# The clamp inside an elu of an elu, moved from VectorE to ScalarE as relu(1 - q)

## The chip, the cores and the metric

The kernel runs on one core of one Trainium2 chip. The metric is the device time of one execution in microseconds (us); three runs of the kernel before gave a median of 2963.7 us (2962.96 to 2964.57). The engines have short names in the profile: PE is TensorE's matmuls, PEld its weight loads, DVE is VectorE, ACT is ScalarE, POOL is GpSimd and SP is SyncE, which only issues transfers.

## The reference

Four graph attention layers run over a batch of 32 graphs with 512 nodes and 256 features. Each layer normalizes its input, takes the relu and adds the attention's result to it. The fourth layer is the one that the change touches. Cut to what matters:

```python
def _gat(inp, adj_mask, W, a):
    ...                                   # leaky relu logits, mask, softmax
    h_prime = jnp.einsum('bij,bjf->bif', att, h)
    return jax.nn.elu(h_prime)
out = jax.nn.relu(jnp.matmul(x, mlp1_w) + mlp1_b)
residual = out
out = _gat(jax.nn.relu(out), None, W_fc, a_fc)
out = jax.nn.elu(out) + residual          # an elu of an elu
out = jax.nn.relu(jnp.matmul(out, mlp2_w) + mlp2_b)
residual = out
out = _gat(jax.nn.relu(out), adj, W_hand, a_hand)
out = jax.nn.elu(out) + residual          # and again
return jax.nn.relu(out)
```

For a positive z, elu(elu(z)) + 1 is z + 1. For a negative z it is exp(exp(z) - 1). Both together are max(z, 0) + exp(min(exp(z), 1) - 1).

## The kernel before

All tensors are fp32 (the adjacency mask is bf16). The 512 nodes of a graph lie in four tiles of 128 partitions. One graph is one batch step, written as a Python generator that goes through the four layers (`layer0` to `layer3`) and yields where it lets another graph in. Four graphs (`NS = 4`, "streams") are in work at once, each a quarter of a batch behind the next, and each owns two of the eight PSUM banks. A planner in Python picks the stream whose next piece is due first (`ready`, `after_us`), and so sets the program order. Then the Tile framework's scheduler, which has its own idea of how long instructions take, sets the order in each engine's queue within the data dependencies. [...]

In the steady part one batch step takes about 89 us of the core, and the order repeats after four batch steps (once for each stream), so there are four variants of a batch period.

The pieces of work that the prediction speaks of, with their lines in the profile:

- `norm`: statistics (L262, L263), reciprocal root on ScalarE (L265, L266), then the normalized tile `xn` on VectorE (L269 where the scale is applied later, L273 where it is applied at once). The matmul helper is L66 and the transpose helper L70. `turn_pair` transposes `xn` and copies it out with a relu (L283).
- `values`: projection matmuls, exponentials of the logits (L312, L315), scaled values `v` (L313 on ScalarE, L316 on VectorE). `weights` then transposes columns of `v` and forms the attention weights on VectorE (L346).
- `averages`: the aggregation matmuls and the reciprocal of the denominator (L364). After it, layer 0 has its elu (exponential L398, relu L399, sums L382 and L383), layer 1 a relu (L417) and an add into `x` (L421).
- layer 2 has four heads (L439, L440, L484, L491, L492).
- layer 3: linear layers (`linear_t`, copied out on ScalarE at L332), the values of the fully connected attention (L515, L516, matmuls with `WFC`). That attention is computed by sorting: rows are scattered (L594), summed up, written to a table and gathered again (L642), which gives `g`, combined on VectorE (L657). Four tiles per batch then take exponential L661, relu L662 and `elu2_plus1`, and are transposed in `mlp_in` and added to `oT` (L713). The last batch takes the plain attention instead (`attend`, L538, L539). The second attention ends with two pairs of tiles, each with exponential L686 and relu L687 twice, `elu2_plus1`, a transpose of `rT`, the sum L697, the relu L698 on ScalarE, and the add into `x` on GpSimd (L700), then the store (L701).

`elu2_plus1(r, q)` receives r = max(z, 0) and q = exp(z), both 128x512, and leaves the sum in r. It has three steps: the clamp (L387, VectorE), the second exponential with the constant -1 as its bias tile (L388, ScalarE), and the add (L389, VectorE). It runs 192 times: 124 times on gathered tiles, 4 times in `attend`, 64 times at the end of layer 3.

Of the kernel before, what the change touches and what calls it, by code (L numbers as in the profile page):

```python
# [19 lines left out]
FP = mybir.dt.float32  # L20
# [3 lines left out]
AF = mybir.ActivationFunctionType  # L24
OP = mybir.AluOpType
# [3 lines left out]
P = 128  # L29
# [6 lines left out]
def fast(ctx, tc, flag, x, adj, w0, a0, w1, a1, w2, a2, mlp1_w, mlp1_b, mlp2_w, mlp2_b,  # L36
         w_fc, a_fc, w_hand, a_hand, out):
    nc = tc.nc
# [12 lines left out]
    const = ctx.enter_context(tc.tile_pool(name="const", bufs=1))  # L51
# [28 lines left out]
    make_identity(nc, ident)  # L80
    eps = const.tile([P, 1], FP, name="eps")
    nc.vector.memset(eps, EPS)
    minus1 = const.tile([P, 1], FP, name="minus1")
    nc.vector.memset(minus1, -1.0)
    seen = const.tile([P, 5 * B], FP, name="seen")

    def load_x(b):
# [296 lines left out]

    def elu2_plus1(r, q):

        nc.vector.tensor_scalar(q, q, 1.0, None, op0=OP.min)  # L387
        nc.scalar.activation(q, q, AF.Exp, bias=minus1)  # L388
        nc.vector.tensor_tensor(r, q, r, op=OP.add)  # L389

    def layer0(xt, xn, rs, when):
# [126 lines left out]
    def attend(oT, b):  # L518
# [12 lines left out]
        for t in range(NT):  # L531
            y, q = pair(), pair("q")
            for c, n in ((0, F + 1), (1, F)):
                ps = bank()
                aggregate(ps[:, :n], wt, t, lambda j: halves[c][:, j, :n])
                if c == 0:
                    rd = reciprocal(ps[:, F:F + 1])
                nc.scalar.activation(q[:, c, :], ps[:, :F], AF.Exp, scale=rd)  # L538
                nc.scalar.activation(y[:, c, :], ps[:, :F], AF.Relu, scale=rd)  # L539
            elu2_plus1(y, q)  # L540
            ys.append(y)
            yield after_us(0)
            if t:
                mlp_in(oT, ys[t - 1], t - 1)
                yield after_us(0)
# [4 lines left out]
    def sort_attend(oT, b):  # L550
# [100 lines left out]
        for t in range(NT):  # L651
            yield landed
            y, q = pair(), pair("q")
            g = gs[t]
            z = g[:, :2 * C]
            tc.keep_in_program_order(
                nc.vector.scalar_tensor_tensor(z, z, ends[:, t, 2:3], g[:, 2 * C:], op0=OP.mult, op1=OP.add)  # L657
            )
            rd = reciprocal(z[:, F:F + 1])
            z = z.rearrange("p (c n) -> p c n", c=2)[:, :, :F]  # L660
            nc.scalar.activation(q, z, AF.Exp, scale=rd)  # L661
            nc.scalar.activation(y, z, AF.Relu, scale=rd)  # L662
            elu2_plus1(y, q)
            if t + 2 < NT:
                gather(t + 2)
            got.append(y)
            landed = after_us(3)
            when.append(after_us(4))
            if t == 0:
                continue  # L670
            yield when[t - 1]
            mlp_in(oT, got[t - 1], t - 1)
# [4 lines left out]
    def layer3(xt, xn, when, b):  # L677
        oT = yield from linear_t((yield from turned(xn, when)), WM1, b1, "oT", 2)
        yield from (attend if b >= B - 1 else sort_attend)(oT, b)
        rT = yield from linear_t(oT, WM2, b2, "rT", 2)  # L680
        v, wt = yield from plain(rT, WHA)
        for t0 in range(0, NT, 2):
            y, q = pair(), pair("q")
            for i in range(2):
                p, rd = averages(v, wt, t0 + i)
                nc.scalar.activation(q[:, i, :], p, AF.Exp, scale=rd)  # L686
                nc.scalar.activation(y[:, i, :], p, AF.Relu, scale=rd)  # L687
                yield after_us(0)
            elu2_plus1(y, q)
            p = bank()  # L690
            for i in range(2):
                for k in range(KF):
                    transpose(
                        p[:, (i * KF + k) * P:(i * KF + k + 1) * P], rT[:, k, (t0 + i) * P:(t0 + i + 1) * P], ident
                    )
            yf = y.rearrange("p a f -> p (a f)")
            nc.vector.scalar_tensor_tensor(yf, p, -1.0, yf, op0=OP.add, op1=OP.add)  # L697
            nc.scalar.activation(y, y, AF.Relu)  # L698
            xr = xt[:, t0:t0 + 2, :]
            nc.gpsimd.tensor_tensor(xr, xr, y, op=OP.add)  # L700
            nc.sync.dma_start(  # L701
                out[b, t0 * P:(t0 + 2) * P, :].rearrange("(t p) f -> p t f", p=P), xr
            )
            yield after_us(0)
# [462 lines left out]
@with_exitstack  # L1167
def kernel(ctx: ExitStack, tc: tile.TileContext, *args):
    nc = tc.nc
    keep = ctx.enter_context(tc.tile_pool(name="keep", bufs=1))  # L1170
    flag = keep.tile([1, 1], I32, name="flag")
    fast(tc, flag, *args)
    bad = nc.values_load(flag[0:1, 0:1], min_val=0, max_val=1)
    with tc.If(bad > 0):
        general(tc, *args)
# [27 lines left out]
```

## Time and profile before

| | before |
|---|---|
| median of 3 runs | 2963.7 us (2962.96 to 2964.57) |
| the profiled execution's own time | 2958.47 us |
| its span in the profile | 2956.8 us |
| mean granted TensorE clock | 0.994 |
| TensorE busy | 2870.2 us, 97% |
| VectorE busy | 2270.1 us, 77% |
| ScalarE busy | 1493.6 us, 51% |
| GpSimd busy | 496.9 us, 17% |

The span is the time from the first to the last instruction; the execution's own time has a little more around it, 1.7 us here. TensorE's busy time is not the same as TensorE at its best, since matmuls overlap and their ends are modelled; the starts of matmuls are recorded. A row of a group of instructions names line, engine, operation, output and inputs, the shape, the count, then the busy time and the mean of one, and the idle time of the engine just before them with what ended it. A row of the waits names who waited for whom, the total in us, how often, and the longest.

### The profile page before, as it was taken

The page shows a single profiled execution, that of the slowest core. Times are in us where ns is not written, and L with a number is a line of the kernel's source. Part 1 is how long each engine was busy: PE and PEld are TensorE (multiplying, and loading weights), DVE is VectorE, ACT ScalarE, POOL GpSimd, SP SyncE. Part 2 cuts the span into 40 slices and gives each one's busy share as a digit, 9 for nine tenths or more (in the row PEclk, how much of TensorE's full clock was granted, in tenths as well). Part 3 has the DMA queues.
Part 4 walks back from the last instruction along what each step waited for, and adds up shares of the span by engine and source line. Part 5 has one row for each costly group of instructions (what it writes and reads, how often), then busy time and mean ns, then how long its engine had stood idle before and what let it go on. Part 6 is the DMA issues. An engine that isn't in the chain of part 4 may idle for free.

```text
span 2956.8 us, 43040 instructions
## 1 busy us (share of the span) xinstructions
PE 2870.2 (97%) x15273; PEld 2335.9 (79%) x15273; DVE 2270.1 (77%) x5674; ACT 1493.6 (51%) x3790; POOL 496.9 (17%) x509
## 2 busy tenths in 40 slices
PE   7999999999999999999999999999999999999998
PEld 6777888778888877888778888778878788887765
DVE  4678878778878778878778778788778788787763
ACT  3444455554555544555544555545555544555444
POOL 0011122111122111122011221111221111221120
PEclk9999999999999999999999999999999999999999
DMA  3022233232232332232222232222232222332230
GB/s 93 18 95 94 81 100 115 82 99 98 83 101 96 99 101 89 83 110 96 99 94 87 87 115 92 96 95 88 91 115 90 96 95 81 101 115 73 93 115 16
DMA packets 192765, 270.88 MB, mean 92 GB/s; under 512 B 16992, under 2 KB 155550, under 8 KB 192544
## 3 DMA queue, kind: packets, MB, share of 16 engines
q1 hardware_dynamic: 162784, 169.76, 18.0%
q0 software_dynamic: 29760, 98.30, 9.8%
q8 instruction: 123, 2.02, 0.3%
q14 instruction: 98, 0.80, 0.1%
HBM read 152.62 MB, written 115.39 MB: 91 GB/s over the span
## 4 chain that ended last, share of the span: by engine, by line
PE 85%; DVE 9%; ACT 3%; issue 2%; DMA 1%; POOL 0%; SPq 0%; POOLq 0%; ACTq 0%; DVEq 0%
PE b L66 77%; PE b L70 8%; DVE st L262 2%; DVE xn L273 1%; DVE xn L269 1%; DVE y L697 1%; DVE v L316 1%; ACT rs L265 1%; DVE y L389 0%; DVE w L346 0%; DVE mv L263 0%; DVE x L421 0%; DVE tot L633 0%; ACT q L388 0%; DMA sums<-order 0%
## 5 line engine op out<-in xcount | busy, mean ns | idle before, releaser
L66 PE MATMUL b<-v,w 128*128 128x65 f32 (+1 forms) x7232 | 1218.1, 321 | 9.7 <-DVE w L346 8.2
L66 PEld LDWEIGHTS b<-v,w 128*128 128x128 f32 x7232 | 1052.9, 191 | 164.9 <-issue 40.8
L66 PE MATMUL b<-WFC,oT 128*128 128x256 f32 (+1 forms) x2048 | 499.7, 381 | 3.0 <-ACT ends L515 3.0
L66 PEld LDWEIGHTS b<-WFC,oT 128*128 128x128 f32 x2048 | 374.1, 190 | 51.3 <-ACT v L516 3.6
L66 PE MATMUL b<-W,hT 128*128 128x259 f32 (+1 forms) x1536 | 384.0, 388 | 0.8 <-DVE v L316 0.3
L346 DVE SCALAR_TENSOR_TENSOR w<-b,v,maskT 128x512 f32<-128x512 f32 x512 | 369.8, 743 | 4.9 <-PE b L70 4.9
L594 POOL DMA_INDIRECT order<-v,at x248 | 280.3, 1130 | 467.5 <-DVE w L346 159.8
L66 PEld LDWEIGHTS b<-W,hT 128*128 128x128 f32 x1536 | 285.7, 192 | 47.0 <-ACT hT L283 2.3
L346 DVE SCALAR_TENSOR_TENSOR w<-spread,v,maskT 128x512 f32<-128x512 f32 x384 | 269.4, 741 | 0.5 <-DMA spread<-row 0.5
L364 DVE RECIPROCAL rden<-b 128x1 f32<-128x1 f32 (+1 forms) x516 | 78.1, 163 | 249.4 <-PE b L66 245.1
L700 POOL TENSOR_TENSOR x<-x,y 128x512 f32<-128x512 f32 x64 | 81.6, 1275 | 1100.4 <-ACT y L698 1040.6
L66 PE MATMUL b<-hT,WM 128*128 128x512 f32 x512 | 250.6, 593 | 1.4 <-ACT hT L283 1.4
L642 POOL DMA_INDIRECT g<-table,at x124 | 120.5, 971 | 735.2 <-ACT y L662 373.6
L66 PE MATMUL b<-oT,WM 128*128 128x512 f32 x512 | 231.7, 595 | 0.0
L516 ACT ACTIVATE v<-b,ends 128x256 f32<-128x256 f32 x256 | 119.4, 466 | 183.9 <-PE b L66 179.0
L262 DVE BATCH_NORM_STATS2 st<-x 128x6 f32<-128x256 f32 x512 | 192.6, 407 | 4.8 <-DMA x<-in_x_dram 2.5
L70 PEld LDWEIGHTS b<-ident,xn 128*128 128x128 f32 x1024 | 125.0, 142 | 70.9 <-DVE xn L273 32.9
L389 DVE TENSOR_TENSOR y<-q,y 128x512 f32<-128x512 f32 x192 | 132.6, 691 | 59.9 <-ACT q L388 58.5
L70 PE MATMUL b<-ident,xn 128*128 128x128 f32 x1024 | 155.2, 278 | 21.9 <-DVE xn L273 16.0
L332 ACT ACTIVATE oT<-b,bias 128x512 f32<-128x512 f32 x128 | 88.3, 690 | 169.8 <-PE b L66 169.8
L66 PEld LDWEIGHTS b<-oT,WM 128*128 128x128 f32 x512 | 97.7, 191 | 96.0 <-issue 92.7
L283 ACT ACTIVATE hT<-b 128x512 f32<-128x512 f32 x256 | 146.7, 591 | 46.4 <-PE b L70 46.3
(141 smaller groups left out, 3759.9 us busy)
## 6 DMA issues: line engine op xcount, KB each, us to landing
table<-sums SPq DMA_DIRECT2D x62, 1032.0 KB
sums<-order SPq DMA_DIRECT2D x62, 516.0 KB
spread<-row SPq DMA_DIRECT2D x96, 256.0 KB
x<-in_x_dram SPq DMA_DIRECT2D x32, 512.0 KB
out_dram<-x SPq DMA_DIRECT2D x64, 256.0 KB
sums<-order SPq DMA_DIRECT2D x62, 129.0 KB
order<-v,at POOLq DMA_INDIRECT x248, 2.8
g<-table,at POOLq DMA_INDIRECT x124, 4.4
```

The source lines that it names most:

```text
L66: nc.tensor.matmul(p, w, x, **flags)
L70: instruction = nc.tensor.transpose(p, x, i)
L262: nc.vector.bn_stats(st[:, i, :], xt[:, t0 + i, :])
L283: nc.scalar.activation(hT[:, :, t0 * P:(t0 + 2) * P], p.rearrange("p (k n) -> p k n", k=KF), AF.Relu)
L332: nc.scalar.activation(o[:, f, :], p, AF.Relu, bias=bias[:, f:f + 1])
L346: w = nc.vector.scalar_tensor_tensor(wt[:, j, :], r, t_col(j), maskT[:, j, :], op0=OP.max, op1=OP.mult)
L364: nc.vector.reciprocal(r, den)
L389: nc.vector.tensor_tensor(r, q, r, op=OP.add)
L516: nc.scalar.activation(halves[c][:, t, :F], ps[:, :F], AF.Copy, scale=ends[:, t, 0:1])
L594: nc.gpsimd.indirect_dma_start(out=orders[c], out_offset=bass.IndirectOffsetOnAxis(ap=at[:, 0, t:t + 1], axis=0), in_=halves[c][:, t, :], ...
L642: nc.gpsimd.indirect_dma_start(out=g, out_offset=None, in_=table, in_offset=bass.IndirectOffsetOnAxis(ap=at[:, 1, t:t + 1], axis=0),)
L700: nc.gpsimd.tensor_tensor(xr, xr, y, op=OP.add)
```

## The change

The clamp min(q, 1) on VectorE goes. In its place ScalarE computes relu(1 - q) with the constant +1 as a bias tile and a scale of -1, and the second exponential takes its input with a scale of -1 and no bias tile: exp(-relu(1 - q)) is exp(min(q, 1) - 1). The constant tile changes from -1 to +1. The add stays.

```diff
-    minus1 = const.tile([P, 1], FP, name="minus1")
-    nc.vector.memset(minus1, -1.0)
+    plus1 = const.tile([P, 1], FP, name="plus1")
+    nc.vector.memset(plus1, 1.0)
...
     def elu2_plus1(r, q):
 
-        nc.vector.tensor_scalar(q, q, 1.0, None, op0=OP.min)
-        nc.scalar.activation(q, q, AF.Exp, bias=minus1)
+        nc.scalar.activation(q, q, AF.Relu, bias=plus1, scale=-1.0)
+        nc.scalar.activation(q, q, AF.Exp, scale=-1.0)
         nc.vector.tensor_tensor(r, q, r, op=OP.add)
```

Since the scheduler weighs the new steps, some neighbouring instructions of other streams change places on TensorE, VectorE, ScalarE and GpSimd too; the order of SyncE's transfers is the same. L387 and L388 are both ScalarE instructions in the changed program.

## The prediction

> **What bounds the kernel now.** I read the busy rows first, then the waits of TensorE and of VectorE, then the timeline around the waits that TensorE shows.
>
> The busy rows (engine, busy us, share of the span):
>
> ```profile
> PE 2870.2 (97%) x15273; PEld 2335.9 (79%) x15273; DVE 2270.1 (77%) x5674; ACT 1493.6 (51%) x3790; POOL 496.9 (17%) x509
> ```
>
> TensorE is the bound and nearly always busy. The change touches VectorE and ScalarE only, so it can move the time only through TensorE's waits. TensorE's own waits (us in total, times, longest):
>
> ```profile
> PE b L70 <- DVE v L316: 25.5, 30, 1.0
> PE b L70 <- DVE xn L273: 16.0, 32, 0.8
> ```
>
> The rest of that list is under 9 us a row, mostly single waits at the start and the end. Read in the timeline from 1456 to 1815 us, four batch periods of about 89.5 us, TensorE pauses at two places in each period: about 1.03 us before the transposes of `v` (for L316; call it V) and before the transposes of `xn` (for L273; call it X), where its matmuls come 0.44 us late in two of four periods and 0.96 us late, with another 0.21 us, in the other two. One further pause is 0.14 us, for the add L389. Everything else that VectorE and ScalarE do has slack. So the question is whether V or X moves.
>
> The waits round the three steps of `elu2_plus1`:
>
> ```profile
> DVE q L387 <- ACT q L661: 48.3, 54, 1.5
> DVE q L387 <- ACT q L686: 38.0, 64, 1.2
> ACT q L388 <- DVE q L387: 1.6, 6, 0.4
> DVE y L389 <- ACT q L388: 58.5, 77, 1.2
> ```
>
> VectorE stands idle for the first exponential, but ScalarE hardly ever waits for the clamp (1.6 us in all): while VectorE clamps, ScalarE runs the plain relu of the same tile (L662 or L687). The clamp is hidden already, and the chain does not get shorter when it goes. The groups that price it (busy us, mean ns; then idle before):
>
> ```profile
> L388 ACT ACTIVATE q<-q,minus 128x512 f32<-128x512 f32 x192 | 137.8, 718 | 5.7 <-DVE q L387 1.6
> L387 DVE TENSOR_SCALAR q<-q 128x512 f32<-128x512 f32 x192 | 83.0, 432 | 97.3 <-ACT q L661 48.3 <-ACT q L686 38.0 <-ACT q L538 10.9
> L491 ACT ACTIVATE q<-y 128x512 f32<-128x512 f32 x64 | 40.3, 630 | 162.7 <-DVE y L484 162.7
> ```
>
> An X place, from the timeline of one period (start us, us):
>
> ```profile
> 1806.48 0.72 ACT L388 ACTIVATE q<-q,minus 128x512 f32<-128x512 f32 x1
> 1807.24 0.69 DVE L389 TENSOR_TENSOR y<-q,y 128x512 f32<-128x512 f32 x1 [0.79 <-ACT q L388]
> ...
> 1809.20 0.69 DVE L697 SCALAR_TENSOR_TENSOR y<-b,y 128x512 f32<-128x512 f32 x1 [0.27 <-PE b L70]
> ...
> 1810.70 1.28 POOL L700 TENSOR_TENSOR x<-x,y 128x512 f32<-128x512 f32 x1 [3.42 <-ACT y L698]
> ...
> 1811.67 0.71 DVE L269 TENSOR_SCALAR xn<-x,mv 128x256 f32<-128x256 f32 x2
> ...
> 1813.79 1.51 DVE L273 TENSOR_SCALAR xn<-x,mv,rs 128x256 f32<-128x256 f32 x4
> ...
> 1814.26 0.33 PE L70 MATMUL b<-ident,xn 128*128 128x128 f32 x1 [0.28 <-DVE xn L273]
> ```
>
> From the add L389 or from L697 on, VectorE works without a gap (L421, L697, the statistics of two norms, L269, L273), and TensorE waits at its end. In the periods with the long pause the same row reads:
>
> ```profile
> 1543.72 1.43 DVE L269 TENSOR_SCALAR xn<-x,mv 128x256 f32<-128x256 f32 x2
> ```
>
> because L700 on GpSimd had started at 1543.48: an L269 that starts between 0.02 us before and 0.97 us after L700 ends only about 1.42 us after L700's start, and the next follows at +1.34 us.
>
> **What the Trainium skill says.** "ScalarE: Activation LUTs", under "What ACT_TABLE_LOAD costs", gives each per-partition pointer operand about 93 ns; the trace agrees (714 ns median for L388 with its bias tile, 630 ns for L491 without). "VectorE: DVE Perf Modes", in "The perf-mode tier table", has an fp32 `tensor_scalar` from SBUF at twice the rate of a `tensor_tensor`: here 427 ns against 692 ns. So the step goes from where it is cheap to where it is dear. "GPSIMD Engine Reference", "1. Specifications", says that GpSimd shares its SBUF interfaces with VectorE's two-port instructions; the 1168 ns of an L269 beside L700, against 345 ns before it, agree.
>
> **The change, part by part.** Removed: 192 clamps of 432 ns, 83.0 us of VectorE (77% to 74%). Added: 192 relus with a pointer, 0.714 us each by L388's own median, 137 us of ScalarE; the second exponential loses its pointer and falls from 714 to 630 ns, minus 16 us. ScalarE gains 121 us, 51% to 55%. The memset of one column is free both ways (one instruction at the start). No DMA is added; SP's order is the same, and on POOL only a gather L642 and an add L700 change places, off TensorE's path (the gather starts several us before its first reader).
>
> The chain gets longer. With S the start of the last exponential from PSUM (L686): before, L687 starts at S+0.37 and L388 ends at S+1.68 (1805.52 to 1807.20). After, relu from S+0.74 to S+1.45, exponential from S+1.49 to S+2.12: the add comes 0.43 us later each time, since both steps wait for their own engine's result. On the gather path (L661, L662) it is +0.6 us; the add there is followed by the transposes of `y` with 0.8 to 9 us to spare in the periods read, except for one place with 0.06 us, where VectorE's own queue, not the exponential, sets the add (L388 ended 0.9 us before it). I cost these at nothing; if that cover failed in each period, it would be 0.3 us times 30, 9 us.
>
> V: the work ahead of it starts from layer 2's reciprocal, after VectorE had waited 2.7 us for TensorE, has no elu of an elu in it, and stands in the same order in both programs. No change.
>
> X: the scheduler reorders, so I followed the orders of the two programs through the four periods.
> - In one period of four (the one shown) the new order puts L332 ahead of the relu, and the reciprocal ahead of the add. L332 can start when its matmul ends, at 1807.04. Relu to 1808.33, exponential to 1809.00, add at 1809.04, L421 at 1809.65, L697 at 1810.25, L698 to 1811.66, L700 at 1811.74; L269 comes at 1811.98, inside L700, so the second starts at 1811.74+1.34 = 1813.08 instead of 1812.04: L273 is 1.04 us later. TensorE's order moves one WFC matmul (0.43 us) ahead of the wait and closes a gap behind it, worth 0.51 us. Net +0.53 us, 7 or 8 times: +4.0 us.
> - In two of four (long pause) the add moves from 1540.78 to 1541.21, L700 to 1543.92, L269 is held as before, and L273 is 0.45 us later. TensorE again has 0.43 to 0.48 us of matmul in front. Net 0.0 (from -0.1 to +0.2).
> - In the fourth the add still ends before the reciprocal that waits for TensorE at 1719.82. Net 0.
>
> The end: the last batch is alone, and three chains lie open there: TensorE waits 0.38 us for L697 at 2943.83 and 0.49 us for L332 at 2930.93, and the output follows the last add. 3 x 0.43 = +1.3 us.
>
> Sum +5.3 us. The profiled execution took 2958.5 us by its clock (span 2956.8), 5.2 us under the median of 2963.7; I take the difference as the same after: 2963.8 profiled, **2969.0 us** median, +0.18%. About 0.2% (5.9 us) is what a measurement of this kernel can tell from no change.
>
> Unknown costs: a relu from SBUF with pointer and scale isn't in the trace; L388's 0.714 us is taken, 0.63 (L698 without pointer) and 0.77 bound it: -0.09 to +0.05 us at each open chain, 3 us over 30. The start of L269 against L700 is known to 0.1 us; ahead of it by some 0.4 us it would be spared the hold (0.75 us less), behind by more it costs up to 0.3 us more.
>
> **Rivals.**
> (1) Faster: the order falls so that L269 passes ahead of L700 in the two long periods. Then 15 X waits shrink by 0.8 us, -12 us, and with the +5.3 us about 2957 us; at the most all X waits go (15 x 0.44 + 15 x 1.17, 24 us) for 2940 us. For it: 83 us of VectorE and 97 us of its blocked time go. Against: L389, in the same queue, waits for the same chain instead.
> (2) Slower: the later L697 moves L698 and L700 on, and L700 holds L269 longer in three periods of four. From L697 0.2 us later than worked out, each period loses 0.4 us more: 23 x 0.4 = +9 us on top of the +5.3, about 2978 us. For it: the trace shows the hold whenever the two meet. Against: the added matmul in front of X absorbs 0.43 us.
> (3) ScalarE's queue becomes late for PSUM buffers: each L399 or L417 behind a relu is 0.6 us later; if one in each period reached TensorE, +18 us on top, 2987 us. Against: 55% busy, and TensorE's waits on ScalarE are 14 us in all, mostly at the ends.
> (4) The change does nothing at all but at the end: 2965 us.
>
> **How the numbers follow.** Likeliest case with (4): 0.50, 2964 to 2973 us alone. (1): 0.17. (2): 0.26. (3): 0.07. Of the first, a tenth lies beyond +0.2%: faster 0.17, same 0.45, slower 0.38. The range 2956 to 2980 us leaves out most of (3) and the far ends of (1) and (2).
>
> **What would show it.** Right: V's row stays 30 waits and about 25 us; X's row grows in count of long pauses (one more period in four); L269 beside L700 stays long in three of four; L387 on ScalarE near 714 ns, L388 near 630; L389's wait for L388 grows from 58.5 us to over 80. Wrong: X's waits shrink (rival 1), or new rows with L399, L417 or L687 before TensorE (rival 3), or V moves.

## The result, and the profile after

The changed kernel takes 2982.8 us (median of four, 2982.34 to 2982.99) beside 2963.3 us for the kernel before (2962.16 to 2964.57): a ratio of 1.0068, 95% interval 1.0055 to 1.0080. It is slower by 19.5 us, where the forecast had +5.3 us and a range up to 2980. The profiled execution took 2982.34 us, its span 2980.6 us, 23.8 us over the span of before.

The busy row of the changed kernel (engine, busy us, share of the span):

```profile
PE 2878.9 (97%) x15273; PEld 2334.3 (78%) x15273; DVE 2192.8 (74%) x5482; ACT 1589.0 (53%) x3982; POOL 505.0 (17%) x509
```

VectorE lost 77 us and ScalarE gained 95 us. The matmuls are the same in number and shape. I held each matmul's start against the median distance between its shape and the shape ahead of it; the starts that come over 0.04 us late sum to 118.1 us before and 142.2 us after. The 24.1 us between them are about the whole difference, so the cost is in TensorE's waits. From TensorE's own waits and from the waits of its weight loads (total us, times, longest):

```profile
PE b L70 <- DVE v L316: 26.1, 30, 1.0
PE b L70 <- DVE xn L273: 19.9, 30, 1.1
PE b L66 <- ACT v L313: 3.8, 1, 3.8
PE b L70 <- DVE y L389: 3.3, 7, 0.5
```

```profile
PEld b L66 <- DVE v L440: 8.9, 23, 0.6
```

The last of these rows in the kernel before:

```profile
PEld b L66 <- DVE v L440: 0.6, 2, 0.4
```

V (L316) stayed. X (L273) grew by 3.9 us. New are the waits for the add L389 before the transposes of `y` (0.6 us before), for L440, which empties the PSUM tile of a `W`,`hT` projection, and one long wait near the end (L313). The groups of the three steps:

```profile
L387 ACT ACTIVATE q<-q,plus 128x512 f32<-128x512 f32 x192 | 137.5, 716 | 0.0
L389 DVE TENSOR_TENSOR y<-q,y 128x512 f32<-128x512 f32 x192 | 132.4, 690 | 154.1 <-ACT q L388 106.9 <-ACT ends L515 46.7
L388 ACT ACTIVATE q<-q 128x512 f32<-128x512 f32 x192 | 120.4, 627 | 1.2
```

VectorE now stands idle for 106.9 us ahead of the add (58.5 us in the kernel before). The cost is not spread evenly. Set against the kernel before at each batch, one batch period of four loses about 1.2 us at the two places shown next, and mostly a further 0.8 to 2.2 us behind them; the other periods differ by some 0.15 us or less. That one is the period shown in the forecast. Its X place in the timeline after (start us, us):

```profile
1462.12 1.27 POOL L700 TENSOR_TENSOR x<-x,y 128x512 f32<-128x512 f32 x1 [4.09 <-DVE mv L263]
1462.43 1.38 DVE L269 TENSOR_SCALAR xn<-x,mv 128x256 f32<-128x256 f32 x2
1465.90 0.33 PE L70 MATMUL b<-ident,xn 128*128 128x128 f32 x1 [1.10 <-DVE xn L273]
```

As worked out, L269 now falls inside L700 and takes 1.38 us for two instead of 0.71. The place that the forecast did not have comes some 5 us later:

```profile
1470.55 0.64 ACT L388 ACTIVATE q<-q 128x512 f32<-128x512 f32 x1
1471.23 2.15 PE L66 MATMUL b<-W,hT 128*128 128x268 f32 x7
1471.29 0.69 DVE L389 TENSOR_TENSOR y<-q,y 128x512 f32<-128x512 f32 x1 [3.62 <-ACT q L388]
1471.90 0.48 DVE L440 SCALAR_TENSOR_TENSOR v<-b,rs,v 128x256 f32<-128x256 f32 x1
1472.43 0.75 PEld L66 LDWEIGHTS b<-W,hT 128*128 128x128 f32 x4 [0.56 <-DVE v L440]
```

Here the add of a gathered tile stands in VectorE's queue in front of L440. VectorE waits 3.62 us for the second exponential, so L440 starts 0.67 us after the row of `W`,`hT` matmuls shown here. In the kernel before it started 0.45 us ahead of them:

```profile
1461.56 0.69 DVE L389 TENSOR_TENSOR y<-q,y 128x512 f32<-128x512 f32 x1 [0.86 <-ACT q L388]
1462.16 0.48 DVE L440 SCALAR_TENSOR_TENSOR v<-b,rs,v 128x256 f32<-128x256 f32 x1
1462.61 2.19 PE L66 MATMUL b<-W,hT 128*128 128x268 f32 x9
```

Two things come together in the changed kernel. L440 also reads what L439 writes on ScalarE, behind the second exponential, and L439 is over only at 1471.35; the add in front of L440 costs some 0.5 us more. The wait also stands in two of the other periods, with 0.32 us, though these periods lose next to nothing: a wait in this list is not yet lost time.

### The profile page after: what moved, and what is told of

Read it like the earlier page. It is cut to its first block, busy times and chain, and to the rows that moved or that the text cites. A ratio compares the mean times of both kernels' runs of the same rounds, so it can differ in the third digit from the quotient of the medians.

```text
span 2980.6 us, 42997 instructions
## 1 busy us (share of the span) xinstructions
PE 2878.9 (97%) x15273; PEld 2334.3 (78%) x15273; DVE 2192.8 (74%) x5482; ACT 1589.0 (53%) x3982; POOL 505.0 (17%) x509
## 4 chain that ended last, share of the span: by engine, by line
PE 76%; DVE 12%; ACT 6%; DMA 3%; issue 3%; POOL 0%; SPq 0%; POOLq 0%; ACTq 0%; DVEq 0%
PE b L66 69%; PE b L70 7%; DVE st L262 2%; DVE xn L269 1%; DMA sums<-order 1%; DVE xn L273 1%; DMA order<-v,at 1%; ACT q L387 1%; DVE y L389 1%; ACT q L388 1%; DVE w L346 1%; DVE v L316 1%; DVE y L697 1%; ACT q L661 1%; DVE mv L263 1%
## 5 line engine op out<-in xcount | busy, mean ns | idle before, releaser
L66 PE MATMUL b<-WFC,oT 128*128 128x256 f32 (+1 forms) x2048 | 492.8, 381 | 3.2 <-ACT v L516 2.9
L642 POOL DMA_INDIRECT g<-table,at x124 | 121.0, 976 | 1613.9 <-DVE rden L364 779.6
L346 DVE SCALAR_TENSOR_TENSOR w<-b,v,maskT 128x512 f32<-128x512 f32 x512 | 371.3, 744 | 6.5 <-PE b L70 6.4
L594 POOL DMA_INDIRECT order<-v,at x248 | 280.3, 1130 | 493.5 <-DVE w L346 192.2
L346 DVE SCALAR_TENSOR_TENSOR w<-spread,v,maskT 128x512 f32<-128x512 f32 x384 | 269.0, 743 | 0.8 <-DMA spread<-row 0.8
L389 DVE TENSOR_TENSOR y<-q,y 128x512 f32<-128x512 f32 x192 | 132.4, 690 | 154.1 <-ACT q L388 106.9
L516 ACT ACTIVATE v<-b,ends 128x256 f32<-128x256 f32 x256 | 119.6, 467 | 156.8 <-PE b L66 154.2
L283 ACT ACTIVATE hT<-b 128x512 f32<-128x512 f32 x256 | 146.5, 591 | 34.7 <-PE b L70 34.5
L686 ACT ACTIVATE q<-b,rden 128x256 f32<-128x256 f32 x128 | 60.5, 473 | 172.1 <-DVE rden L364 172.1
```

Of the source, the lines that this page charges most:

```text
L66: nc.tensor.matmul(p, w, x, **flags)
L283: nc.scalar.activation(hT[:, :, t0 * P:(t0 + 2) * P], p.rearrange("p (k n) -> p k n", k=KF), AF.Relu)
L346: w = nc.vector.scalar_tensor_tensor(wt[:, j, :], r, t_col(j), maskT[:, j, :], op0=OP.max, op1=OP.mult)
L516: nc.scalar.activation(halves[c][:, t, :F], ps[:, :F], AF.Copy, scale=ends[:, t, 0:1])
L594: nc.gpsimd.indirect_dma_start(out=orders[c], out_offset=bass.IndirectOffsetOnAxis(ap=at[:, 0, t:t + 1], axis=0), in_=halves[c][:, t, :], ...
L642: nc.gpsimd.indirect_dma_start(out=g, out_offset=None, in_=table, in_offset=bass.IndirectOffsetOnAxis(ap=at[:, 1, t:t + 1], axis=0),)
```

## The experiments

All times stand beside runs of the kernel before on the same chip, whose median was 2960.2 to 2962.1 us. Where a kernel has a new function, later line numbers are 5 to 9 higher than in the kernel before; the text gives the old number too.

**Which site: the relu only at layer 3's end.** `elu2_new` has the changed kernel's three steps.

```diff
-            elu2_plus1(y, q)          # layer 3's end
+            elu2_new(y, q)
```

> The relu(1 - q) on ScalarE only at the end of layer 3 (64 of 192); the gathered tiles and the plain attention keep the clamp on VectorE. Theory A (the longer chain from the second exponential to the add delays the norm and the transposes of xn, X): X as in the changed kernel, +4 us, and the end of the last batch, so +5 to +9 us over before, whose median was 2963.3. Theory B (one more ScalarE step per gathered tile makes ScalarE late for PSUM tiles that TensorE waits for): B's waits, 10 to 15 us, are missing here, so A's share is all there is, under +9 us. Theory C (what costs is only the order that the scheduler settles on): the sum has no relation to the share of the edit, and could be +20 us or below nothing.

Measured 2964.5 us, ratio 1.0012 (1.0004 to 1.0020), some +3.6 us. The late starts at X went from 20.5 to 24.8 us, as in the changed kernel; the growth is all in one period of four (+0.81 us each).

**Which site: the relu only on the gathered tiles and in `attend`.**

```diff
-            elu2_plus1(y, q)          # sort_attend and attend
+            elu2_new(y, q)
```

> The relu(1 - q) on ScalarE only on the gathered tiles and in the plain attention (128 of 192); the end of layer 3 keeps the clamp on VectorE. Theory A: X stays at before's 20.5 us of late matmuls, and the time within 3 us of before. Theory B: the new waits before the matmuls of W with hT (for L440), the transposes of v (for L312) and of y (for L389) stay, +10 to +15 us, X +1 us at most. Theory C: no relation to the share.

Measured 2977.8 us, ratio 1.0060 (1.0046 to 1.0074). X stayed at 20.6 us. The two sites add up: 0.12% and 0.60% against 0.68% for both. The gathered tiles, which the forecast had costed at nothing, carry about four fifths of the loss.

**ScalarE's time by itself, badly placed.** A spare relu after every add, reading a constant tile:

```diff
         nc.vector.tensor_tensor(r, q, r, op=OP.add)
+        nc.scalar.activation(spare, spare, AF.Relu)   # 128x416
```

> Before's three steps, and after each add one further relu of 128x416 bf16 on ScalarE on a spare tile that nobody reads: about 0.5 us each, 192 times, some 100 us of ScalarE, with no longer chain. Theory A: within 3 us of before. Theory B: ScalarE is late for PSUM tiles as in the changed kernel, new rows of waits for L440, L312, L399 or L389, +10 to +20 us. Theory C: no relation.

Measured 2973.5 us, ratio 1.0036 (1.0023 to 1.0050), but this tells nothing on the theories. Nothing tied the spare relus to their tiles, and the scheduler put most of them first. The busy time of the instructions that touch the spare tile in the first 150 us (limits and length of the stretch, then busy us and count on VectorE and ScalarE, the granted clock, DMA):

```profile
0.00:150.00 150.00, 0.41 (x1) 93.69 (x172) 0.92 0.18 52
```

Of the 192 spare relus 172 stand here. The kernel is 12.5 us late at 144 us, where the first batch's gathered rows are marked, and 12.9 us after thirty batches, so the steady part lost 0.5 us; the end lost a further 4 us.

**ScalarE's time, tied to the tile but off the chain.** The spare relu reads `q` behind the second exponential, in the gathered tiles and `attend` alone. First 0.44 us from one start to the next:

```diff
         nc.scalar.activation(q, q, AF.Exp, bias=minus1)
+        nc.scalar.activation(spare, q[..., :416], AF.Relu)
         nc.vector.tensor_tensor(r, q, r, op=OP.add)
```

> Gathered tiles and plain attention only: before's three steps, and one further relu on ScalarE that reads 128x416 of q behind the second exponential into a spare tile nobody reads. ScalarE's queue gets a step of about 0.5 us where the changed kernel has its relu, and the add's chain is no longer than before. Queue theory (ScalarE is late for PSUM tiles that TensorE waits for): the late starts of W with hT after themselves, 5.5 us before and 10.5 us with the change on the gathered tiles alone, come back at 9 us or more, and the time is +8 to +12 us over before. Chain theory (the add comes late and the transposes of y wait): within 3 us of before.

Measured 2962.5 us, ratio 1.0002 (0.9994 to 1.0010). Then with the bias tile as a third operand, 0.53 us, which is what the change adds per tile:

```diff
+        nc.scalar.activation(spare, q[..., :416], AF.Relu, bias=minus1)
```

> As the kernel with the spare relu of 128x416 on the gathered tiles and the plain attention, but the spare relu takes the bias tile, so that ScalarE's step is about 0.09 us longer: 0.53 us from the start of one instruction to the next instead of 0.44, the same as the changed kernel adds per gathered tile (a relu of 0.61 less 0.09 that the exponential loses). The add's chain stays that of before. Queue theory with a slack of about 0.45 us in one period of four: the wait of W with hT for L440's counterpart appears (0.1 to 0.3 us), the one of the transposes of v for L312's stays near 0.35 us: +2 to +6 us over before. If the late PSUM tiles need the longer chain too: within 2 us of before, as with 0.44 us.

Measured 2962.7 us, ratio 1.0002 (0.9993 to 1.0010). And two of them:

> Two of these spare relus per gathered tile, 1.06 us of ScalarE's queue each time, the add's chain as before. Queue theory: past its slack of about 0.45 us each further 0.1 us comes out as 0.1 us of TensorE's waits wherever a PSUM tile is released behind it, at least at three places in one period of four: 3 x 0.6 us x 8 = +14 us, and more if the other periods' slack is used up too (up to +60 us). If ScalarE's queue has slack that the traces do not show: under +5 us.

Measured 2964.9 us, ratio 1.0010 (1.0002 to 1.0018). The queue theory had about 14 us for two steps. As the main cause ScalarE's queue fell: a step as long as the change's costs nothing that can be told apart, twice as much 3 us. Two of its waits did appear. The late starts of the transposes of `v` behind one another rose from 0.4 us to between 2.3 and 3.0 us, waiting for L312. And with two spare relus the wait for L440 (here L449) is back, in one period of four, where L440 stands waiting for L439 behind both of them on ScalarE:

```profile
PEld b L66 <- DVE v L449: 4.9, 10, 0.5
```

**The same ScalarE time on the chain.** The further relu now works on `q` in place, so that the add waits for it; the exponential is positive and the value stays.

```diff
         nc.scalar.activation(q, q, AF.Exp, bias=minus1)
+        nc.scalar.activation(q, q, AF.Relu)
         nc.vector.tensor_tensor(r, q, r, op=OP.add)
```

> Gathered tiles and plain attention only: before's three steps, and between the second exponential and the add one further relu of q in place on ScalarE (0.52 us from one start to the next; exp is positive, so the value stays). The same occupancy of ScalarE as the spare relu that cost 0.9 us, but on the chain to the add. Chain theory (the add, in VectorE's in-order queue, comes later, and L440 behind it frees its PSUM tile later than TensorE asks for it): waits of W with hT for L440's counterpart come back, and +10 to +17 us over before, near the +15.7 us of the change on these tiles. Occupancy theory: +1 us, as off the chain.

Measured 2968.6 us, ratio 1.0028 (1.0017 to 1.0040), +8.3 us: clear of the occupancy theory, and short of the 10 to 17 us of the chain theory. With two of them:

> Two such relus on the chain. Chain theory: each step behind the add comes 0.5 us later again; if nothing is rearranged +20 to +40 us, but the scheduler sees the longer chain and may place the transposes of y and the add later, which would keep it near the +10 to +17 us of one. Occupancy theory: +3 us, as with two off the chain.

Measured 2982.5 us, ratio 1.0082 (1.0069 to 1.0096). In one table, time over before (ratio less 1 times 2962 us):

| ScalarE's further step per gathered tile | off the chain | on the chain |
|---|---|---|
| about 0.52 us | +0.6 us (-2.1 to +3.0) | +8.3 us (+5.0 to +11.8) |
| about 1.05 us | +3.0 us (+0.6 to +5.3) | +24 us (+20 to +28) |

The pair at 0.52 us can be read in the timeline, since ScalarE's order up to L439 and L312 is the same in both at this place. The off-chain kernel (L397 is the add L389, L448 is L440):

```profile
1461.13 0.69 DVE L397 TENSOR_TENSOR y<-q,y 128x512 f32<-128x512 f32 x1 [0.86 <-ACT q L395]
1461.40 0.64 ACT L396 ACTIVATE spare<-q,minus 128x416 bf16<-128x416 f32 x1
1462.18 2.19 PE L66 MATMUL b<-W,hT 128*128 128x268 f32 x9
1462.24 0.48 DVE L448 SCALAR_TENSOR_TENSOR v<-b,rs,v 128x256 f32<-128x256 f32 x1 [0.42 <-ACT v L447]
```

The on-chain kernel (L396 is the add, L447 is L440):

```profile
1465.60 0.62 ACT L395 ACTIVATE q<-q 128x512 f32<-128x512 f32 x1
1466.32 0.69 DVE L396 TENSOR_TENSOR y<-q,y 128x512 f32<-128x512 f32 x1 [1.87 <-ACT q L395]
1466.38 1.81 PE L66 MATMUL b<-W,hT 128*128 128x268 f32 x6
1466.93 0.48 DVE L447 SCALAR_TENSOR_TENSOR v<-b,rs,v 128x256 f32<-128x256 f32 x1
1467.47 0.52 PEld L66 LDWEIGHTS b<-W,hT 128*128 128x128 f32 x3 [0.45 <-DVE v L447]
```

The further step starts 0.78 us ahead of the matmuls in both. Off the chain the add is over at 1461.82, and L440's counterpart starts 0.06 us after the matmuls; on the chain it stands behind the add and starts 0.55 us after them, and the weight loads wait. So ScalarE's step alone used up L440's lead of 0.45 us, and the add then made it late. Over the whole run the weight loads wait 0.6 us (2 times) for it off the chain and 6.8 us (16 times) on it.

**No clamp at all, everywhere.** Since exp(exp(z) - 1) is at least z + 1, clamping can be left to the add:

```diff
-        nc.vector.tensor_scalar(q, q, 1.0, None, op0=OP.min)
         nc.scalar.activation(q, q, AF.Exp, bias=minus1)
-        nc.vector.tensor_tensor(r, q, r, op=OP.add)
+        nc.vector.scalar_tensor_tensor(r, r, 1.0, q, op0=OP.add, op1=OP.min)
```

> No clamp on either engine: the second exponential is taken of the unclamped q with the bias -1, and the add becomes min(r + 1, exp(q - 1)), one step on VectorE, which is the same value since exp(e^z - 1) is at least z + 1. VectorE loses 83 us and ScalarE gains nothing, so it shows the half of the change that removes, without the half that adds. If a lighter VectorE shortens TensorE's waits (rival 1 of the forecast): X shrinks by 5 to 15 us and the time is 2948 to 2958 us. If the clamp was hidden (theories A and B, where only the added ScalarE step matters): within 4 us of 2963. Theory C: off from before by over 5 us without a new queue of work anywhere.

Measured 2958.8 us, ratio 0.9988 (0.9981 to 0.9995). X shrank from 20.5 to 17.6 us, but the late starts of the transposes of `y` grew from 1.3 to 7.5 us, although nothing had been added. The time lies between the two expectations and decides for neither, so I split this form by site too.

**No clamp on the gathered tiles alone** (the same edit there).

> The form without the clamp (add as min(r + 1, exp(q - 1))) on the gathered tiles and the plain attention alone; layer 3's end as before. VectorE loses 55 us, ScalarE gains nothing, the chain to the add is no longer. Order theory (the scheduler, seeing a shorter chain, puts the transposes of y two matmuls earlier in one period of four, while the add on VectorE still stands behind a reciprocal that waits for TensorE): the wait for y grows from 0.14 to 1.1 us there, 8 x 0.95 us = +7 us, though work only goes. Work theory (less on VectorE and no more on ScalarE cannot cost): within 2 us of before, or faster.

Measured 2966.2 us, ratio 1.0014 (1.0008 to 1.0021): slower by 4 us by removing work, a little over half of what the order theory had. Its timeline in the period with the wait (L393 is the second exponential, L394 the add):

```profile
1489.21 0.71 ACT L393 ACTIVATE q<-q,minus 128x512 f32<-128x512 f32 x1
1491.57 0.18 DVE L364 RECIPROCAL rden<-b 128x4 f32<-128x4 f32 x1 [2.04 <-PE b L66]
1492.13 0.68 DVE L394 SCALAR_TENSOR_TENSOR y<-y,q 128x512 f32<-128x512 f32 x1
1492.87 0.66 PE L70 MATMUL b<-ident,y 128*128 128x128 f32 x4 [0.84 <-DVE y L394]
```

The exponential is over at 1489.92, 2.2 us before the add. The add waits for nothing of its own: VectorE keeps to the order of its queue and stands idle for 2.04 us, since the reciprocal in front of the add waits for TensorE. The scheduler had moved the transposes two matmuls of `v` and `w` ahead. The changed kernel has those two matmuls moved in the same way, the same reciprocal in front of its add (1498.11, add 1498.67, second exponential over at 1497.77) and a late start of 0.69 us there, 0.14 us before. So this part of the loss, 3.9 us, comes from the order, not from the add's inputs. Why the scheduler moves them in both was not shown; the chain is shorter in the one and longer in the other.

**No clamp at layer 3's end alone.**

> At layer 3's end alone (64 of 192) no clamp, and the add as min(r + 1, exp(q - 1)); the gathered tiles as before. In the kernel with this form everywhere the long pause before the transposes of xn fell from 0.96 + 0.21 us to 0.75 us in two of four periods, and the transposes of y waited 1.08 us instead of 0.14 us in one of four. If both are local effects of their sites: X falls by 0.43 us 15 times, the wait for y stays at 0.14 us: -6 to -7 us, 2955 to 2957 beside a before of 2962. If they are one effect of the scheduler's order: near the -3.3 us of the form everywhere.

Measured 2954.0 us, ratio 0.9975 (0.9964 to 0.9985), as the local reading said. VectorE's queue now has L697 ahead of L421, L700 starts earlier against the norm, and L269 starts 0.97 us after it instead of 0.24: two take 0.71 us instead of 1.43. This is the gain that the forecast's rival (1) had, got by another edit and in another way: L269 starts late in L700, not ahead of it.

**The hold of L269 beside L700, priced.** The changed kernel without the last add into `x`:

```diff
-            nc.gpsimd.tensor_tensor(xr, xr, y, op=OP.add)
...
-                out[b, ...], xr
+                out[b, ...], y
```

> The changed kernel without the add into x on GpSimd (L700): the store writes y, so the last residual is left out of the output. It prices the hold of L269 beside L700, which the forecast's sum at X rests on. If the hold makes the long pauses: L269 falls from 1111 or 1430 ns to about 350 ns wherever it met L700, the pause before the transposes of xn falls by about 0.75 us in three of four periods, 23 x 0.75 = 17 us, to about 2965 us. If the hold is hidden behind something else at X: within 4 us of the changed kernel's 2982.8.

Measured 2959.8 us, 0.9993 of before (0.9986 to 0.9999), so about 22 us under the changed kernel; X's late starts fell from 24.8 to 7.6 us, 17.2 us where 17 was expected; the other 5 us or so were not taken apart. L269's group (behind the first bar its busy us and the mean ns of one) in the changed kernel and without the add:

```profile
L269 DVE TENSOR_SCALAR xn<-x,mv 128x256 f32<-128x256 f32 x256 | 95.0, 410 | 0.0
```

```profile
L269 DVE TENSOR_SCALAR xn<-x,mv 128x256 f32<-128x256 f32 x256 | 77.6, 342 | 0.0
```

**A version that beats both.** No clamp at layer 3's end, and L700 on VectorE:

```diff
-            nc.gpsimd.tensor_tensor(xr, xr, y, op=OP.add)
+            nc.vector.tensor_tensor(xr, xr, y, op=OP.add)
```

> The fastest form so far (no clamp at layer 3's end, min in the add, measured 2954.0) with the last add into x (L700) on VectorE instead of GpSimd, 64 adds of about 0.69 us. The hold of L269 goes (0.66 to 0.75 us at two of four periods' X), but the add stands in VectorE's queue and waits for L698 on ScalarE. If the scheduler puts it behind the norm's steps: X falls by 0.75 us 15 times, -11 us, 2943. If it stands before L269 and L273: X grows by the add and by the wait for L698 (0.6 to 1.4 us) in all four: +18 to +30 us, 2972 to 2984.

Measured 2947.7 us, ratio 0.9952 (0.9939 to 0.9966), the fastest here. In a period that had the long pause (L705 is L700):

```profile
1536.72 0.66 DVE L705 TENSOR_TENSOR x<-x,y 128x512 f32<-128x512 f32 x1
1537.39 0.58 DVE L269 TENSOR_SCALAR xn<-x,mv 128x256 f32<-128x256 f32 x2
```

Both branches of the expectation were half right. The add does stand before L269 and costs about 0.6 us there, but L698 was done by then, and the hold is gone in every period. The first late start falls to 0.36 us in two of four periods and vanishes in the other two; 0.21 us on the next transpose is now in all four. X's own sum is 5.8 us, and the late transposes of `xn` behind one another went from 5.2 to 11.3 us. The kernel gains 6.3 us over the form with L700 on GpSimd, not 11.

**The clamp on GpSimd, on the gathered tiles alone.**

```diff
-        nc.vector.tensor_scalar(q, q, 1.0, None, op0=OP.min)
+        nc.gpsimd.tensor_scalar(q, q, 1.0, None, op0=OP.min)
```

> Gathered tiles and plain attention only: the clamp min(q, 1) on GpSimd. The chain to the add gets longer by more than in the changed kernel (the 128x512 add L700 takes 1.28 us there), and ScalarE's queue gets nothing. Queue theory: late starts of W with hT stay at 5.5 us and those of the transposes of v after themselves at 0.4 us; what is left is the wait for the add before the transposes of y, 0.5 to 1.5 us in one period of four: +2 to +10 us. Chain theory: at least the +15.7 us that the change on these tiles costs, since the chain is longer.

Measured 3180.6 us, ratio 1.0737 (1.0722 to 1.0752), far from both expectations. I had meant it as a longer chain with nothing in ScalarE's queue. It wasn't: ScalarE stood still for the clamp, 212.2 us in all (L393, the exponential behind it is L394):

```profile
ACT q L394 <- POOL q L393: 212.2, 120, 7.0
```

```profile
PE b L66 <- ACT y L405: 95.4, 23, 6.4
```

L405 is layer 0's relu L399, which frees PSUM tiles and stood behind that exponential. GpSimd's own queue also holds the scattering and gathering transfers (L594, L642), about 1.1 and 1.0 us each, and the clamp took 1.49 us; how the wait splits between these was not taken apart. TensorE paid twice: around most of the long waits the trace shows its granted clock at half, mostly for 3.4 to 6.8 us (240 us in all, 38 us in the kernel before; mean clock 0.963 against 0.994), and there the 257-column matmuls of `v`,`w` start 427 ns apart instead of 216. The late starts of under 1 us in these stretches sum to 83 us, against 10 us before.

## Why the prediction was wrong

Late starts of TensorE by place (those over 0.06 us each), in us over the whole run, from the traces:

| place | before | changed | relu, layer 3's end | relu, gathered | off chain, 0.53 | on chain, 0.52 | no clamp, gathered |
|---|---|---|---|---|---|---|---|
| `xn` after `WFC` (X) | 20.5 | 24.8 | 24.8 | 20.6 | 20.6 | 20.6 | 20.6 |
| `W`,`hT` after itself | 5.5 | 11.7 | 7.1 | 10.5 | 7.1 | 10.3 | 6.8 |
| `v` transposes after themselves | 0.4 | 3.1 | 0.7 | 3.2 | 3.0 | 2.8 | 0.3 |
| `y` transposes after `v`,`w` | 1.3 | 5.2 | 1.4 | 5.3 | 1.6 | 0.5 | 7.3 |
| `v`,`w` after itself | 7.6 | 9.9 | 8.2 | 9.4 | 7.7 | 10.4 | 9.3 |
| one `WHA`,`rT` near the end | 0.3 | 4.0 | 2.9 | 3.4 | 3.3 | 0.3 | 0.3 |

- **V, right.** 30 waits of 26.1 us, 25.5 before.
- **X, right in its mechanism; the close sum is in part luck.** "+0.53 us, 7 or 8 times: +4.0 us" measured +4.3 us in late starts. The chain in that period came as worked out to within 0.1 us up to L269, but the late start there grew by 0.82 us, seven times, and not by 0.53: L273 was a further 0.2 us late since L266, the root on ScalarE, stood behind L516. Each of the other three periods gave 0.06 or 0.07 us back (forecast 0.0), which brought the sum down again.
- **The durations, right; their sum on ScalarE, too high.** L387 took 716 ns (714), L388 627 ns (630), but ScalarE's busy time grew by 95 us and not 121: neighbours overlap, and starts lie 0.61 us apart where one lasts 0.71, so 192 x (0.61 - 0.09) = 100 us.
- **The failed step** is the gather path: "I cost these at nothing; if that cover failed in each period, it would be 0.3 us times 30, 9 us." The gathered tiles alone measured 17.8 us (13.6 to 21.9), the end included. The step looked only at the readers of the add, the transposes of `y`. It didn't ask what stood behind the add in VectorE's queue. It also saw the one place with 0.06 us to spare and left it at nothing, though the new order has the transposes of `y` two matmuls earlier there. The chain also grew by more than the +0.6 us given: from the start of the gathered exponential L661 to the add it is 2.05 us before (1459.51 to 1461.56) and 3.05 us after (1468.24 to 1471.29), since a copy-out L283 now runs between relu and second exponential. L440 behind the add then releases its PSUM tile late. That it is the chain to the add, and not ScalarE's time, is shown by steps of one length on and off it: 8.3 against 0.6 us, and 24 against 3.0 us. How much of it goes through L440 is not shown. At 0.52 us its wait is there on the chain and absent off it, but in the table `W`,`hT` is 3.2 us and `v`,`w` 2.7 us higher on the chain, each kernel has its own order elsewhere, and with two steps off the chain L440's wait is back (4.9 us) while the kernel loses 3.0 us.
- **What else the gathered tiles cost.** ScalarE's queue ahead of L312: +2.8 us, which appears off the chain too. The moved transposes of `y`: +3.9 us, which appears without any added work. `v`,`w` waiting for L399 behind L388: about +2 us, seen in the trace and not tested alone.
- **Rival (3)** had the place, PSUM tiles freed late, and nearly the size (18 us), at a chance of 0.07. It named ScalarE's queue; by the table that queue has some 3 to 5 us, and the larger share goes to VectorE's queue (`W`,`hT`, +5.0 us) and to the order (`y`, +4.0 us). The split is not clean, since L439 on ScalarE takes part in the wait for L440.
- **The end, mis-sized.** Forecast +1.3 us; from 2723 us of the run before to the end 4.8 us were lost, 2.4 with layer 3's end alone and 2.3 with the gathered tiles alone. The open chains came nearly as forecast: in the last batch `WHA`,`rT` waits 0.37 us longer and `v`,`w` 0.56 us longer for L697, both with layer 3's end alone too. Not forecast were a wait of 1.4 us after the transposes of `ends` in `attend`, for L352 (also with the gathered tiles alone), and a moved wait of `WHA`,`rT` for L313, the table's last row, which in part takes the place of a 2.5 us wait for L346 a few us later. That one comes and goes with the order in kernels with quite different edits; what decides it stays open.

## What to carry to other kernels

When a step gets later, look not only at who reads its result but at every instruction behind it in its own engine's queue, and find those that release a PSUM tile: here one add late by 1 us held L440, and TensorE waited. ScalarE, at 51%, took a step of 0.5 us per tile for nearly nothing off the chain (0.6 us); on the chain to the add the same step cost 8.3 us. And where a scheduler orders by its own durations, even removing work can cost (4 us here): compare the orders around each wait that has less slack than the move.

## What was unexpected of the hardware

A one-input clamp of 128x512 fp32 took GpSimd 1492 ns (median of 128), longer than its own two-input add L700 (1275 ns) and 3.5 times VectorE's 432 ns. The Trainium skill, in "GPSIMD Engine Reference", "4.1 Engine selection", calls one-input operations there "roughly line-rate" and two-input ones about twice as slow; for this operation the trace says otherwise. The hold of L269 agrees in the main with "SBUF — State Buffer", "Who interferes with whom", which says that of a VectorE instruction in a two-port mode and a GpSimd instruction whoever issues first locks the other out: with L700 gone from GpSimd, L269's mean fell to 342 ns and to 337 ns with the add on VectorE, where the same add takes 677 ns instead of 1275. One point differs: in the kernel before, eight L269 start 0.02 us ahead of their L700 by the recorded start times, and it is these that are held, to 1.43 us, while L700 takes its usual 1.27 us.
